# Four residual layers on one core: the start and end of the third stage written out as a list, and two bias additions moved in the first

## The chip, the core and the metric

The kernel runs on one core of one Trainium2 chip. The metric is the device time of one execution in microseconds, the median of several runs. Matmuls run on TensorE (PE), elementwise work on VectorE (DVE), ScalarE (ACT) and GpSimd (POOL), and SyncE (SP) issues most transfers; POOL issues some too.

## The reference

The input x has shape (8192, 8, 16, 16) in fp32. Four layers each add to x a linear map of its group norm (four groups of channels for every sample):

```
x = x + tt_matvec([core0, core1, core2], gn(x)) + bias0             # layer 0
x = x + relu(batchnorm(conv3x3(gn(x)) + bias1))                     # layer 1
g = gn(x);  sx = 127 / max|g|;  sw = 127 / max|w2|
x = x + conv3x3(round(g * sx), round(w2 * sw)) / (sx * sw) + bias2  # layer 2
x = x + conv3x3(edge_pad(gn(x)), sign(w3) * mean|w3|) + bias3       # layer 3
```

Layer 0 is a product of three small cores of rank 8 instead of a full matrix. The batch norm of layer 1 and the largest magnitude in layer 2 need all samples, so there are two points at which everything must be known.

## The kernel before

A tile is 128 samples, so there are 64 tiles (`NT`), each of 128 rows with 2048 values. The two global results cut the work into three stages: the first does layer 0 and the convolution of layer 1 for tile after tile, the second applies the batch norm and finds the largest magnitude, the third does layers 2 and 3. Most of the intermediate tiles go through DRAM between stages; `KEEP` = 13 stay on chip in slots.

PE, DVE, ACT and POOL are called through `InOrder` (line 43), which keeps each engine's instructions in the order in which the Python code issues them. So the order written in the kernel is the order on every engine, nearly all of the rows of the profile carry line 43, and a step that waits holds up whatever stands behind it on its engine.

**The first stage** goes through quarters of tiles: a loop over n = 4t + q. Layer 0 of a quarter is an expansion on PE (`pu`), its copy by ACT (`u`), and the main product on PE (`po`), which DVE adds to the tile (`xs`). The transposed operand of the expansion arrives in two parts, a rounded one (`xh`, by ACT) and the rest (`bs - xh`, by POOL); `limbs(t, q)` makes both and sends them to DRAM (`limb_d`), and `fetch(t, q)`, a transfer that POOL issues, brings them back as `xl`. Around the matmuls of quarter n the loop hangs other steps into slots 0 to 6 with `at(slot, condition, step, ...)`: norms of tiles to come, layer 1 of tiles gone by, and `add_bias(t)`, one POOL addition of bias 0 over the whole tile (128 x 2048). That addition must come before the first `po` of tile t is added to it. For tile 1 it is in quarter 0, for tile 2 in slot 5 of quarter 1, for tile t + 3 in slot 1 of the last quarter of tile t. DVE meanwhile also builds the weights of the later layers (`ys`, `band`, `sign`, `wsum` and others).

**The third stage** is one loop over laps in which eight tiles are under way at different steps. For a tile the steps are, in their order: `rows2` (DVE: the norm's factors as rows) and `spread` (PE: spread over the columns into `ps_a`), `scale2` (DVE: `v`, as int8), `round2` (ACT: `q`, as bf16), `bias2` (ACT, on the first half of x), `layer2` (PE: two halves `pq`; DVE adds the first to x, ACT scales the second into `z` and POOL adds that), `square3` (ACT: `sq`), `stats3` (PE: `s`; DVE: `s_d`, `mv`; POOL: a power of `mv`), `rows3` and `spread` again (`ps_r`, `ps_o`), `offset3` (ACT: `c`), `scale3` (DVE: `t`, in the buffers `sq` and `xh`), `high3` (ACT: `hi` with its edges), `low3` (POOL: `lo` = t - hi, then x + c), `edges3` (ACT), `layer3` (PE: two halves `pf`, each six matmuls with hi and six with lo) and `finish` (DVE; after the second half SP issues the store). In a lap i these steps are called for tiles i + 3 to i - 3 in a fixed sequence, whose start and end are the same lap with the tiles that do not exist left out. The tile that a lap loads from DRAM is i + 7 (`AHEAD`).

Of the kernel before, what the change touches and what calls it, by code (L numbers as in the profile page):

```python
# [18 lines left out]
P = 128  # L19
# [13 lines left out]
class InOrder:  # L33
# [5 lines left out]
    def __getattr__(self, name):  # L39
        op = getattr(self.engine, name)  # L40

        def call(*args, **kwargs):
            return self.tc.keep_in_program_order(op(*args, **kwargs))  # L43
        return call

# [6 lines left out]
def tile_net(ctx: ExitStack, tc: tile.TileContext, xb, xt_in, pack0, pack1, pack2, out):  # L54
# [210 lines left out]
    def samples(t):  # L265
        return t.rearrange("p (b w) -> p b w", w=W)
# [29 lines left out]
    with first as s:  # L296
# [274 lines left out]
        for n in range(NT * NQ):  # L571
            t, q = divmod(n, NQ)
            steps = {}

            def at(r, ok, f, *args):
                if ok:
                    steps.setdefault(r, []).append((f, args))

            def at1(r, f, lag):
                if quarter_of(n, lag):  # L580
                    at(r, True, f, *quarter_of(n, lag))

            last, before, ahead = t == NT - 1, t > 0, t + 2 < NT
            if n > 0:
                next(rest, None)
                if n == 1:
                    next(rest, None)
            tn, qn = divmod(n + 1, NQ)
            at(0, tn < NT, expand, tn, qn, 0)
            at(4, tn < NT, expand, tn, qn, 1)  # L590
            at1(0, conv1_input, LAG)
            if n < NT * NQ - 1:
                at1(6, conv1_scaled, LAG - 1)
            if n == 0 and NT > 1:
                at(1, True, norm_b_spread, 1)
                at(1, True, norm_b_apply, 1)
                at(1, True, add_bias, 1)
            if q == 0:
                if before and t - 1 not in y_of:
                    nc.sync.dma_start(x1_d[t - 1], T[t - 1]["x"])  # L600
                at(1, before, norm_sums, t - 1)
                at(4, before, norm_stats, t - 1)
                if ahead:
                    load_b(t + 2)
            elif q == 1:
                at(1, ahead, norm_b_square, t + 2)
                at(1, before, norm_apply, t - 1)
                at(4, t + 3 < NT, load_t, t + 3)
            elif q == 2:
                at(1, ahead, norm_b_sums, t + 2)  # L610
                at(1, ahead, norm_b_stats, t + 2)
            else:
                at(1, t + 3 < NT, add_bias, t + 3)
                at(1, ahead, norm_b_spread, t + 2)
                at(1, ahead, norm_b_apply, t + 2)
            at1(3, conv1_output, LAG + 1)

            for m in {0: [], 1: [4, 5], 2: [6, 7], 3: []}.get(n, [n + NQ]):
                at(0 if n < 3 else 2, m < NT * NQ, limbs, *divmod(m, NQ))
            for m in {0: [], 1: [4, 5], 2: []}.get(n, [n + 3]):  # L620
                at(5, m < NT * NQ, fetch, *divmod(m, NQ))
            if n == 1:
                at(5, NT > 2, add_bias, 2)
            if last:
                at(2, q > 1, quarter_apply, t, q - 2)
                at(2, q > 0, quarter_stats, t, q - 1)
            main(t, q, steps, n0=QS // 2 if n == 0 else None)
            if quarter_of(n, LAG):
                conv1(*quarter_of(n, LAG))
            if n == NT * NQ - 2 and NT > STAY + 3:  # L630
                load2(STAY)
                load2(STAY + 1)
# [47 lines left out]
    def sums_pe(ps, x, sq):  # L680

        for k, src in ((0, x), (1, sq)):
            for q in range(NQ):
                pe.matmul(ps[32 * q:32 * q + 32], L["wsum"][:, k], src[:, q * BANK:(q + 1) * BANK],
                          start=(k == 0), stop=(k == 1))
# [5 lines left out]
    def stats_small(mv, st, ps, name):  # L691

        s = small.tile([P, 32], F32, name=f"s_{name}", tag="s")
        dve.tensor_reduce(s, samples(ps), AX.X, ALU.add)
        dve.transpose(st, s)
        sq = small.tile([P, G], F32, name=f"sq_{name}", tag="sqm")
        dve.tensor_copy(mv[:, 0:G], st[:, 0:G])
        dve.tensor_tensor(sq, st[:, 0:G], mv[:, 0:G], ALU.mult)
        dve.scalar_tensor_tensor(mv[:, G:2 * G], st[:, G:2 * G], EPS, sq, ALU.add, ALU.subtract)
# [144 lines left out]
    with ExitStack() as s:  # L844
# [5 lines left out]
        sq3, t3, z3 = sqs[0], [sqs[1], xh], [y_stay[3][:, h * F // 2:(h + 1) * F // 2] for h in range(2)]  # L850
        T = [dict() for _ in range(NT)]
        AHEAD = min(NT, KEEP - 6)
        FIRST = 3
        diag2, diag3 = diagonal("d"), diagonal("e")

        ps_a, ps_r, ps_o = (ps_s.tile([P, BANK], F32, name=f"ps_{n}", tag=n) for n in ("a", "r", "o"))
# [4 lines left out]
        def load3(i):  # L861
            t = order[i]
            if t in kept:
                T[i]["x"] = kept[t]
                return
            T[i]["x"] = x_slots[(NT - KEEP + i) % KEEP]
            nc.sync.dma_start(T[i]["x"], x2_d[t])

        def halves(t):
            return t.rearrange("p (h n) -> p h n", h=2)  # L870
# [7 lines left out]
            dve.tensor_tensor(mr, st3[:, 0:G], mv[:, G:2 * G], ALU.mult)  # L878
            T[i]["rows3"] = to_rows(diag3[i % 2], mask, [mr, mv[:, G:2 * G], gnst[:, order[i], 0:G]], f"e{i}")

        def spread(i2, i3):

            if 0 <= i2 < NT:
                pe.matmul(r2, L["sel0"], T[i2].pop("rows2"), start=True, stop=True)
            if 0 <= i3 < NT:
                rows = T[i3].pop("rows3")
                pe.matmul(r3, L["sel1"], rows, start=True, stop=True)
                pe.matmul(o3, L["corr"], rows, start=True, stop=True)

        def scale2(i):  # L890

# [15 lines left out]
        def layer2(i, h):  # L907
            pc = ps_c.tile([P, 2, BANK], F32, name=f"pq_{i}_{h}", tag="pc")
            for k in range(2):
                pv, xv = samples(pc[:, k]), samples(T[i]["q"])[:, (2 * h + k) * QS:(2 * h + k + 1) * QS]  # L910
                pe.matmul(pv, L["band2"][:, 1], xv, start=True, stop=False)
                pe.matmul(pv[:, :, 1:W], L["band2"][:, 0], xv[:, :, 0:W - 1], start=False, stop=False)
                pe.matmul(pv[:, :, 0:W - 1], L["band2"][:, 2], xv[:, :, 1:W], start=False, stop=True)
            pc, x = pc.rearrange("p k n -> p (k n)"), halves(T[i]["x"])[:, h]
            if h == 0:
                dve.scalar_tensor_tensor(x, pc, inv, x, ALU.mult, ALU.add)
            else:
                z = z3[i % 2]
                act.activation(z, pc, AF.Identity, bias=L["bias2"], scale=inv)
                pool.tensor_tensor(x, x, z, ALU.add)  # L920

        def square3(i):
            act.activation(sq3, T[i]["x"], AF.Square)

        def stats3(i):
            ps = ps_s.tile([P, BANK], F32, name=f"s3_{i}", tag="s3")
            sums_pe(ps, T[i]["x"], sq3)
            T[i]["mv"] = small.tile([P, 2 * G], F32, name=f"mv3_{i}", tag="mv")
            stats_small(T[i]["mv"], st3, ps, f"d{i}")
            stats_pow(T[i]["mv"])  # L930

        def offset3(i):
# [19 lines left out]
        def low3(i):  # L952
            hi = T[i]["hi"]
            T[i]["lo"] = lo = wk.tile([P, P, W + 2], F32R, name=f"lo_{i}", tag="lo")
            pool.tensor_tensor(lo[:, :, 1:W + 1], samples(T[i].pop("t")), hi[:, :, 1:W + 1].bitcast(F32), ALU.subtract)
            x = samples(T[i]["x"])
            pool.tensor_tensor(x, x, over_w(T[i].pop("c"), 0, P), ALU.add)

# [14 lines left out]
        def finish(i, h):  # L973
            x = halves(T[i]["x"])[:, h]
            pc = T[i].pop(("pf", h)).rearrange("p k n -> p (k n)")
            dve.scalar_tensor_tensor(x, pc, L["scale3"], x, ALU.mult, ALU.add)
            if h == 1:
                nc.sync.dma_start(out[order[i]], T[i]["x"])
                T[i].clear()

        def at(i, f, *args):
            if 0 <= i < NT:
                f(i, *args)

        for i in range(AHEAD):
            load3(i)
        for i in range(-FIRST, NT + 4):
            at(i + AHEAD, lambda j: j >= AHEAD and load3(j))
            at(i + FIRST, rows2)
            at(i - 1, rows3)  # L990
            at(i - 3, finish, 1)
            at(i, square3)
            at(i + 1, layer2, 0)
            spread(i + FIRST, i - 1)
            at(i - 1, offset3)
            at(i + 1, layer2, 1)
            at(i + FIRST, scale2)
            at(i, stats3)
            at(i - 1, scale3)
            at(i - 2, edges3)  # L1000
            at(i + 2, round2)
            at(i - 1, high3)
            at(i + 2, bias2)
            at(i - 1, low3)
            at(i - 2, layer3, 0)
            at(i - 2, finish, 0)
            at(i - 2, layer3, 1)


# [67 lines left out]
```

## Time and profile before

| what | value |
| --- | --- |
| median of 4 runs | 3845.68 us (3844.68 to 3848.49) |
| profiled execution | 3845.59 us |
| its span | 3843.8 us |
| granted TensorE clock, mean | 0.96 |
| first stage | 0 to about 2607 us |
| second stage | about 2620 to 3070 us |
| third stage | 3070.3 to 3843.8 us |
| PE busy, 130 to 2600 us | all of 2470.0 us |
| PE busy, 3070 to 3123 us | 36.5 of 53.0 us |
| PE busy, 3123 to 3800 us | 673.9 of 677.0 us |
| PE busy, 3800 to 3843.8 us | 34.6 of 43.8 us |

The span is what the hardware profiler saw between the first and the last instruction; the time of the execution lies 1.8 us above it. In the lines of a view the first number is when an instruction starts, in microseconds from the beginning of the span, and the second how long it takes; a name in front of an arrow is what is written, and those behind it are what is read. In brackets stands idle time of the engine just before, with what ended it. `pf` and `po` are the large matmul groups. A row joins neighbouring instructions of one kind where it says x2 or more.

### The profile page before, as it was taken

How to read it: one execution, taken by the hardware profiler on the slowest of the kernel's cores; microseconds unless marked ns; L12 is line 12 of the kernel's file. 1: busy time of each engine (PE TensorE's matmuls, PEld its weight loads, DVE VectorE, ACT ScalarE, POOL GpSimd, SP SyncE). 2: the span in 40 equal slices, each digit the busy share in tenths (PEclk: the TensorE clock that was granted, in tenths of full speed). 3: DMA queues.
4: the chain of work that ended last, by engine and by line, in shares of the span. 5: the costliest groups of instructions: out<-in, count | busy, mean ns of one | idle time of the engine just before them, and what ended most of it. 6: DMA issues, size and time to landing. Idle time of an engine off the chain costs nothing.

```text
span 3843.8 us, 52765 instructions
## 1 busy us (share of the span) xinstructions
PE 3606.2 (94%) x16264; PEld 2126.8 (55%) x16326; DVE 3403.3 (89%) x6313; ACT 2510.9 (65%) x2676; POOL 3049.7 (79%) x3104
## 2 busy tenths in 40 slices
PE   7999999999999999999999999996665589999999
PEld 4666666666666666666666666662211145555555
DVE  8988888888888888888888888877998889999997
ACT  5666666666666666666666666665665477777775
POOL 4877778777777787777877777766887679999998
PEclk9999999999999999999999999997776699999999
DMA  5787787877877878778788887757999624444432
GB/s 211 243 278 256 261 266 250 271 254 263 268 256 261 260 256 275 255 260 267 251 269 253 263 269 257 251 170 307 425 425 425 266 100 185 178 185 187 175 154 99
DMA packets 210809, 960.93 MB, mean 250 GB/s; under 512 B 44896, under 2 KB 45152, under 8 KB 110048
## 3 DMA queue, kind: packets, MB, share of 16 engines
q1 hardware_dynamic: 173808, 692.22, 48.5%
q0 software_dynamic: 36288, 264.26, 23.2%
q8 instruction: 131, 2.15, 0.2%
q14 instruction: 150, 1.23, 0.1%
q10 hardware_dynamic: 432, 1.08, 0.1%
HBM read 578.84 MB, written 378.54 MB: 249 GB/s over the span
## 4 chain that ended last, share of the span: by engine, by line
PE 85%; DVE 7%; DMA 5%; POOL 2%; issue 1%; ACT 0%; POOLq 0%; SPq 0%; DVEq 0%; ACTq 0%
PE po L43 44%; PE pu L43 12%; PE pf L43 10%; PE pm L43 6%; PE pq L43 4%; PE s L43 3%; PE pc L43 3%; DVE top L43 2%; DMA sq<-y_d 1%; DVE ys L43 1%; DMA xs<-x_d 1%; DMA ys<-x_d 1%; DMA u<-x_d 1%; DMA xk<-x_d 1%; DMA x_d<-xs 1%
## 5 line engine op out<-in xcount | busy, mean ns | idle before, releaser
L43 PE MATMUL po<-u,core 128*128 128x512 f32 (+1 forms) x4112 | 1844.0, 591 | 1.7 <-DVE xs L43 1.7
L43 ACT COPY u<-pu 128x2048 f32<-128x2048 f32 x512 | 955.4, 1866 | 514.2 <-PE pu L43 514.0
L43 PEld LDWEIGHTS po<-u,core 128*128 128x128 f32 x4112 | 744.2, 190 | 738.6 <-issue 735.9
L43 PE MATMUL pu<-core2r,xl 128*128 128x256 f32 x4032 | 678.5, 310 | 5.3 <-ACT u L43 4.7
L43 PEld LDWEIGHTS pu<-core2r,xl 128*128 128x128 f32 x4032 | 527.9, 189 | 128.6 <-issue 122.0
L43 POOL TENSOR_TENSOR bs<-bs,xh 128x512 fp32r<-128x512 f32 (+1 forms) x253 | 325.4, 1287 | 203.9 <-ACT xh L43 203.7
L43 POOL TENSOR_TENSOR v<-e 128x128 f32<-128x128 f32 x750 | 396.7, 540 | 0.0
L43 DVE TENSOR_TENSOR xs<-po,xs 128x512 f32<-128x512 f32 x256 | 176.9, 691 | 216.8 <-PE po L43 216.7
L43 ACT ACTIVATE m<-pm,b 128x128 f32<-128x128 f32 x250 | 91.7, 367 | 390.6 <-PE pm L43 390.6
L43 PEld LDWEIGHTS pm<-v,fast 128*128 128x128 f32 x2000 | 262.5, 191 | 119.7 <-issue 107.1
L43 POOL TENSOR_TENSOR e<-x1n,x 128x512 f32<-128x512 f32 x250 | 305.8, 1223 | 23.5 <-ACT x L43 16.0
L43 DVE TENSOR_TENSOR bs<-bs,stat 128x1024 f32<-128x1024 f32 x252 | 290.8, 1217 | 2.1
L43 POOL TENSOR_TENSOR xs<-xs,w 128x2048 f32<-128x2048 f32 x64 | 291.9, 4560 | 0.6 <-DMA xs<-in_xt 0.6
L43 PE MATMUL pm<-v,fast 128*128 128x128 f32 x2000 | 263.5, 275 | 0.0
L43 ACT ACTIVATE x<-x1n 128x512 f32<-128x512 f32 x500 | 247.0, 545 | 2.1 <-DVE x1n L43 2.1
L43 POOL TENSOR_TENSOR mv<-mv,mhalf 128x4 f32<-128x4 f32 x127 | 130.8, 1030 | 139.5 <-DVE mv L43 139.5
L43 PE MATMUL pf<-hi,sign 128*128 128x512 f32 x768 | 227.6, 434 | 0.0
L43 POOL DMA_DIRECT2D xl<-limb_d x252 | 149.8, 594 | 95.5 <-ACT x L43 25.6
L43 PE MATMUL pf<-lo,sign 128*128 128x512 f32 x768 | 220.2, 424 | 2.0 <-ACT lo L43 2.0
L43 POOL TENSOR_TENSOR v<-r 128x128 f32<-128x128 f32 x500 | 215.1, 446 | 0.0
L43 ACT ACTIVATE sq<-xs 128x2048 f32<-128x2048 f32 x103 | 196.7, 1910 | 11.0 <-DVE xs L43 6.3
L43 PE MATMUL gb<-rows_c,sel 128*128 128x128 f32 x128 | 40.5, 411 | 169.0 <-DVE rows_c L43 169.0
(293 smaller groups left out, 7206.5 us busy)
## 6 DMA issues: line engine op xcount, KB each, us to landing
xl<-limb_d POOLq DMA_DIRECT2D x252, 1024.0 KB, 7.4
x_d<-xs SPq DMA_DIRECT2D x76, 1024.0 KB, 8.4
xs<-in_xt SPq DMA_DIRECT2D x64, 1024.0 KB, 7.5
bs<-in_xb SPq DMA_DIRECT2D x63, 1024.0 KB, 5.7
limb_d<-xh SPq DMA_DIRECT2D x1008, 64.0 KB, 4.4
limb_d<-bs SPq DMA_DIRECT2D x1008, 64.0 KB, 5.2
y_d<-ys SPq DMA_DIRECT2D x60, 1024.0 KB, 8.1
u<-x_d SPq DMA_DIRECT2D x36, 1024.0 KB, 6.2
```

Source lines behind the costliest of these rows:

```text
L43: return self.tc.keep_in_program_order(op(*args, **kwargs))
```

## The change

It has two parts.

In the third stage the fixed loop is replaced by a list of pairs (step, tile). Some steps are cut in two so that they can be placed by themselves: `spread` becomes `spread2` and `spread3`; `layer2` leaves the DVE addition to `first2` (in the list `stz`), ACT's part to `second2` (`z1`) and POOL's to `add2` (`add1`); `stats3` becomes `sums3`, `stats3` (`small`) and `pow3`; the second addition of `low3` becomes `add3` (`corr`). The list's middle is `TURN`, the sequence of the lap before. Its first entries are replaced by `C_HEAD`, in which the tiles 0 to 8 occur, and its last ones by `C_TAIL`, in which the tiles are counted from the end. Each step is in the list as often as before.

In the first stage `add_bias(2)` goes from slot 5 of quarter 1 to slot 2 of quarter 4, and `add_bias(3)` from slot 1 of quarter 3 to slot 5 of quarter 5, behind `fetch`.

```diff
+C_HEAD = """
+rows2:0 rows2:1 spread2:0 v:0 rows2:2 spread2:1 bias:0 v:1 q:0 rows2:3 spread2:2 v:2 c2h1:0 c2h0:0 stz:0 spread2:3
+q:1 z1:0 add1:0 v:3 bias:1 c2h0:1 sq:0 c2h1:1 stz:1 z1:1 sums:0 rows2:4 small:0 add1:1 pow:0 spread2:4 rows2:6
+rows3:0 q:2 q:3 sq:1 c2h1:2 c2h0:2 spread3:0 sums:1 z1:2 bias:2 rows2:5 t:0 small:1 hi:0 stz:2 c:0 add1:2 pow:1
+c2h1:3 rows3:1 spread3:1 c2h0:3 v:4 sq:2 lo:0 z1:3 t:1 bias:3 corr:0 sums:2 stz:3 edl:0 hi:1 c:1 small:2 q:4
+spread2:5 c3h0:0 out0:0 c3h1:0 c2h1:4 v:5 add1:3 pow:2 sq:3 rows3:2 out1:0 lo:1 rows2:7 z1:4 spread3:2 t:2 bias:4
...
+C_TAIL = """
...
+add1:-1 out1:-4 out0:-4 hi:-3 sq:-1 c:-3 spread3:-2 sums:-1 lo:-3 corr:-3 c:-2 t:-2 edl:-3 c3h0:-3 small:-1 c3h1:-3
+pow:-1 hi:-2 lo:-2 rows3:-1 out0:-3 spread3:-1 t:-1 edl:-2 hi:-1 c3h0:-2 corr:-2 lo:-1 edl:-1 c:-1 corr:-1 out1:-3
+out0:-2 c3h1:-2 out1:-2 c3h0:-1 out0:-1 c3h1:-1 out1:-1
+""".split()
...
-                at(1, t + 3 < NT, add_bias, t + 3)
+                at(1, before and t + 3 < NT, add_bias, t + 3)
...
-            if n == 1:
-                at(5, NT > 2, add_bias, 2)
+
+            at(2, n == NQ and NT > 2, add_bias, 2)
+            at(5, n == NQ + 1 and NT > 3, add_bias, 3)
...
+        TURN = [("rows2", 3), ("rows3", -1), ("out1", -3), ("sq", 0), ("c2h0", 1), ("stz", 1), ("spread2", 3), ("spread3", -1),
+                ("c", -1), ("c2h1", 1), ("z1", 1), ("add1", 1), ("v", 3), ("sums", 0), ("small", 0), ("pow", 0), ("t", -1),
+                ("edl", -2), ("q", 2), ("hi", -1), ("bias", 2), ("lo", -1), ("corr", -1), ("c3h0", -2), ("out0", -2),
+                ("c3h1", -2)]
+        todo = [(op, i + k) for i in range(-3, NT + 4) for op, k in TURN if 0 <= i + k < NT]
+        if len(todo) >= len(C_HEAD) + len(C_TAIL):
+            head, tail = ([(op, int(i) + n) for op, i in (c.split(":") for c in l)] for l, n in ((C_HEAD, 0), (C_TAIL, NT)))
+            todo = head + todo[len(head):len(todo) - len(tail)] + tail
         for i in range(AHEAD):
             load3(i)
-        for i in range(-FIRST, NT + 4):
-            at(i + AHEAD, lambda j: j >= AHEAD and load3(j))
...
+        for op, i in todo:
+            if op == "rows2" and AHEAD <= i + 4 < NT:
+                load3(i + 4)
+            OPS[op](i)
```

## The prediction

> **What bounds the kernel now.** I read the page's first and fourth parts, then the chain of waits and the timeline where the diff touches: the first 110 us, the start and the end of the third stage.
>
> ```profile
> PE 3606.2 (94%) x16264; PEld 2126.8 (55%) x16326; DVE 3403.3 (89%) x6313; ACT 2510.9 (65%) x2676; POOL 3049.7 (79%) x3104
> ...
> PE 85%; DVE 7%; DMA 5%; POOL 2%; issue 1%; ACT 0%; POOLq 0%; SPq 0%; DVEq 0%; ACTq 0%
> ```
>
> TensorE is 94% busy, and 85% of the chain. So only places where PE is not the chain are open to a new order. The first is the start of stage one, where the chain of waits runs on DVE from about 40 to 97 us:
>
> ```profile
> 50.48 4.63 DVE mvb L43
> ...
> 57.07 4.80 DVE ys L43
> ...
> 96.88 3.70 PE po L43 x8
> ```
>
> The timeline shows what those two DVE steps are (start, duration, engine, operation):
>
> ```profile
> 48.03 4.60 POOL L43 TENSOR_TENSOR xs<-xs,w 128x2048 f32<-128x2048 f32 x1
> ...
> 50.48 4.62 DVE L43 TENSOR_SCALAR mvb<-mvb 128x8 f32<-128x8 f32 x1
> ...
> 56.60 4.84 POOL L43 TENSOR_TENSOR xs<-xs,w 128x2048 f32<-128x2048 f32 x1
> ...
> 57.07 4.79 DVE L43 TENSOR_TENSOR ys<-ys 128x384 f32<-128x384 f32 x1
> ```
>
> The same TENSOR_SCALAR takes 0.17 us at 95.65, and another ys of this shape 0.56 at 61.89. Both stand still beside POOL work on SBUF: `add_bias(2)` at 48.03 with two limb subtractions behind it, and `add_bias(3)` at 56.60. Ten microseconds on, PE pays:
>
> ```profile
> 68.61 1.91 ACT L43 ACTIVATE sq<-xs 128x2048 f32<-128x2048 f32 x1 [6.33 <-DVE xs L43]
> ...
> 70.94 1.86 ACT L43 COPY u<-pu 128x2048 f32<-128x2048 f32 x1
> ...
> 72.85 2.08 PE L43 MATMUL pu<-core2r,xl 128*128 128x256 f32 x8 [4.71 <-ACT u L43]
> ...
> 74.72 4.90 PE L43 MATMUL po<-u,core 128*128 128x512 f32 x8
> ```
>
> DVE's late xs holds ACT's sq, that holds the u copy, PE idles 4.71 us and then runs slow: 2.08 and 4.90 for groups that take 1.50 and 3.60 around 60 us.
>
> The second place is the start of stage three, at the reduction `pm` (3070.33); "+" below counts from there.
>
> ```profile
> 3077.75 1.44 PE L43 MATMUL pq<-q,band 128*128 128x512 bf16 x3 [0.76 <-ACT q L43]
> ...
> 3082.44 1.20 ACT L43 ACTIVATE bs<-pq,bias,inv 128x1024 f32<-128x1024 f32 x1 [3.69 <-PE pq L43]
> ...
> 3083.55 1.89 ACT L43 CAST q<-v 128x2048 bf16<-128x2048 int8 x1
> ...
> 3085.48 2.72 PE L43 MATMUL pq<-q,band 128*128 128x512 bf16 x6 [3.14 <-ACT q L43]
> ...
> 3111.00 1.82 PE L43 MATMUL pf<-hi,sign 128*128 128x512 f32 x6
> ```
>
> ACT's q of tile 1 stands behind the z of tile 0, which waits 3.69 for PE; then PE waits 3.14 for q. From 3111.00 the pf matmuls run and soon a lap takes 11.54 us (PE: ps 0.67, pq 2.7, s 1.85, pf 6.4). The third place is the drain, where POOL rows follow one another:
>
> ```profile
> 3819.60 4.28 POOL L43 TENSOR_TENSOR lo<-sq,hi 128x2048 fp32r<-128x2048 f32 x1 [0.52 <-POOL mv L43]
> ...
> 3823.83 3.69 POOL L43 TENSOR_TENSOR xk<-xk,c 128x2048 f32<-128x2048 f32 x1
> ...
> 3827.49 4.28 POOL L43 TENSOR_TENSOR lo<-xh,hi 128x2048 fp32r<-128x2048 f32 x1
> ...
> 3831.71 3.70 POOL L43 TENSOR_TENSOR ys<-ys,c 128x2048 f32<-128x2048 f32 x1
> ```
>
> **The steady laps: nothing.** `TURN` is the old loop's order with its pieces named, and the engines keep it; the same matmuls, casts and transfers are issued, `load3(i+4)` still with `rows2(i)`. What hides it is PE's 11.54 per lap; POOL's lap (lo 4.27, c 3.69, half 2.42, pow 1.02 = 11.40) is next, 0.14 below. A new start can't change the pitch of lists that wait only on each other, and I saw no stretched DVE row in stage three.
>
> **Stage one: 4.0 us less.** Taking the two adds out of the first tile gives DVE back 4.62 - 0.17 = 4.45 and 4.79 - 0.56 = 4.23: 8.68 us, all on the chain. Part is lost where they are put.
>
> `add_bias(2)` now follows the limb subtraction that POOL did at 71.12. That one waits for ACT's cast, and ACT comes forward less than DVE: its u copy at 60.42 (1.87) stays, then sq 1.91, cast 0.60, POOL's subtraction 1.26: the add runs from about 66.1 to 70.6. DVE's next scalar step of that kind (mv, at 76.47 before) comes 8.7 earlier, at 67.8, and stands 2.8 us. POOL's pow of mv is queued behind the add, but needs that mv anyway.
>
> `add_bias(3)` follows the fetch at 80.87 (0.57 on POOL's queue, so the add would start at 81.44). DVE's copy to `sign` ran at 81.35 for 0.36: a lead of 0.1 us. If the copy wins, nothing is held; if the add is first, DVE stands most of 4.55, some 4.5. Queued behind the add on POOL are e, r and v of the first 3x3 convolution (85.35 before, after 3.91 us of idle time, waiting for ACT): covered unless they come over 3 us earlier.
>
> So DVE's chain gains 8.68 - 2.8 = 5.9, or 1.4 with the copy held. PE's own loss there was 4.71 + 0.58 + 1.30 = 6.6, so it does not cap this much. The middle is 3.7; I take 4.0, as the slow PE groups (1.88) go in both cases. From 97 us on the steady 10.08 us quarters are PE's and carry the shift on.
>
> The Trainium skill (SBUF — State Buffer, Who interferes with whom) says that a GpSimd instruction and a VectorE instruction with two SBUF inputs, or in a two-port mode, exclude each other for the whole length of whichever is first. The 4.79 row agrees, and by it a move saves nothing by itself: the add takes its toll from whatever stands beside it at the new place.
>
> **Start of stage three: 3.9 us less.** What is moved: `rows2` and `spread2` of tiles 1 and 2, v(1) and bias(0) come before the first pq, and q(1) before z(0).
> - First pq. v(0) ends near +5.5 (3.03 + 2.35); v(1) +6.7 to +9.05 as before; `spread2(2)` writes the bank that v(1) reads, and PE holds the pq behind it: +9.5, where before had +7.42. That is 2.1 lost. ACT's bias(0) (1.14) ahead of q(0) ends it at +8.5, covered.
> - Then the four halves of tiles 0 and 1 run without the 3.14 and 3.69 waits: with 8 matmuls at 0.43 and 16 at 0.22 plus one ps_a, PE is through at +17.2.
> - z(0) after the first half (+12.1) 1.2, POOL's half 2.4 to +15.7, sq 1.9 to +17.6, second half of s 1.03: +18.7. Before: 3092.07 + 1.03 = 3093.10, +22.8. Gain 4.1.
> - From there to the first pf before took 17.9 us, of which s_d to lo's edge is some 13.5 on the rows (1.7, pow 1.07, 1.1, t 2.34, hi 2.47, lo 4.27, 0.54). POOL's half of tile 1 (2.4) now stands before pow of tile 0, beside s_d. I keep 17.9, and take 0.2 off for slow s matmuls: 3.9.
>
> The bounds come from the clock. Its view by windows gives 0.50 for 3076.4 to 3081.1, 1.00 to 3084.5 and 0.50 to 3091.3. All 24 first matmuls at 0.43 cost 16 x 0.21 = 3.4 more, gain 0.5; if the 6.4 us of PE waits between 3093 and 3111 shrink by a quarter, gain 5.5.
>
> The Trainium skill (TensorE: Matmul & The Clock Gate, Part 1) says that half speed is given up only after a busy window of about 3.4 us, that the windows run freely, and that the count of slow matmuls varies by run. The stretches of 3.4 us agree; by that rule either end can occur in one run or another.
>
> **Drain: 0.1 us less.** The last 25.23 us of POOL (3810.18 to 3835.41: lo, c, pow, lo, c, lo, c) hold 0.52 of idle time, and `C_TAIL` leaves them in this order. At most 0.5 can go; nothing follows but ACT's edge, pf 4.93, DVE 1.28 and the last store.
>
> Sum: 4.0 + 3.9 + 0.1 = 8.0. The profiled execution took 3845.59 (span 3843.8 and 1.8 around it), 0.09 below the median of four (3845.68): 3845.59 - 8.0 = 3837.6. About 0.2%, 7.7 us, is what a measurement of this kernel tells from no change, so "faster" is below 3838.0, and my forecast sits on the border.
>
> **Rivals.**
> - *Half given back.* The add beats the copy (1.4 instead of 4.0) and the first matmuls stay slow (0.5 instead of 3.9), or one of them with the other part poor: 2 to 5 us in all, 3840.6 to 3843.6. For: a lead of 0.1 us, and half clock in three of the first four windows. Against: PE in the new head has work queued without a break from +9.5.
> - *Fuller gain.* The copy wins (5.9) and the waits up to the first pf shrink (5.5): 11.4, 3834.2. For: 13.5 against 17.9. Against: in-order POOL gets the half of tiles 1 and 2 between.
> - *Slower: late fetches.* The fetches of xl at 98.53 and 109.20 have no cover: the latter lands in 7.65, at 116.85, and PE's pu starts at 116.99. If the moved adds push POOL's queue past its idle time, each add costs PE 4.55 and a slow group like the one at 72.85 (1.9). One add: stage one +6.5 instead of -4.0, with 4.0 gained in stage three a total of +2.5, 3848.1; both: 12.9 - 4.0, 3854.5. It decides when POOL falls behind by more than its waits at 71.12 (9.11), 77.11 (4.74) and 85.35 (3.91), 17.8 us for 9.1 us of adds: unlikely.
> - *It does nothing.* Stage three has no gain if the first pf stays at +40.7 after all; this falls into the first rival, with 3841.5.
>
> **How the numbers follow.** Forecast 0.58 (its own range 3835.5 to 3840.5; 0.38 below 3838.0 and 0.20 above); half given back, with nothing in stage three, 0.20; fuller gain 0.14; late fetches 0.08, of which 0.05 for both adds. Faster 0.38 + 0.14 = 0.52; slower 0.05; same 0.43. The range 3834.0 to 3843.6 leaves out the slower rival, and an edge on either side.
>
> **What would show it.** Right: no DVE row of 4.6 near 50 and 57 us; PE's 4.71 gone; one mv row of about 3 us under the add at 66 to 71; first pf at about +36.8 after the reduction with the first pq at about +9.5; laps of 11.54; the last POOL rows with the same order and spacing. Wrong: a `sign` row over 4 us, a PE wait on xl of microseconds near 100 to 117, laps that differ, or a drain shorter by over 0.5.

## The result

| | before | changed |
| --- | --- | --- |
| median | 3846.12 us (60 runs, 3842.89 to 3848.49) | 3841.78 us (42 runs, 3839.85 to 3845.57) |
| profiled execution, span | 3845.59, 3843.8 us | 3842.75, 3841.0 us |

The changed kernel is 4.3 us faster: the ratio is 0.999 with a 95% interval of 0.9985 to 0.9994, or 2.3 to 5.8 us. The forecast was 3837.6, 8.0 us faster, which lies outside that interval; the measured time lies inside the forecast's range, at the rival called "half given back" (3840.6 to 3843.6). In the terms of the prediction it is "same", less than 7.7 us; with over a hundred runs in the comparison it is nonetheless clear of zero.

The page of the changed kernel, its first and fourth parts, shows how small that is beside the whole:

```profile
PE 3604.7 (94%) x16264; PEld 2127.2 (55%) x16326; DVE 3399.7 (89%) x6313; ACT 2512.4 (65%) x2676; POOL 3048.4 (79%) x3104
...
PE 85%; DVE 6%; DMA 6%; issue 2%; POOL 1%; ACT 1%; POOLq 0%; SPq 0%; DVEq 0%; ACTq 0%
```

**First stage.** The chain of waits of the changed kernel, 40 to 130 us, no longer holds mvb and ys at four to five microseconds. Two other DVE rows stand there, and the transfers follow:

```profile
67.95 2.46 DVE mv L43
...
75.10 4.86 DVE sign L43
...
83.86 1.76 ACT u L43
...
107.10 7.84 DMA xl<-limb_d
```

The timeline of the same stretch shows both additions at their new places and who stands beside them:

```profile
65.83 4.53 POOL L43 TENSOR_TENSOR xs<-xs,w 128x2048 f32<-128x2048 f32 x1
...
67.95 2.45 DVE L43 TENSOR_SCALAR mv<-mv 128x8 f32<-128x8 f32 x1
...
73.34 1.32 POOL L43 TENSOR_TENSOR bs<-bs,xh 128x512 fp32r<-128x512 f32 x1 [0.84 <-ACT xh L43]
...
73.56 1.51 DVE L43 TENSOR_TENSOR band<-ys 128x384 f32<-128x384 f32 x1
...
74.60 0.57 POOL L43 DMA_DIRECT2D xl<-limb_d  x1
75.10 4.86 DVE L43 CAST sign<-band 128x384 fp32r<-128x384 f32 x1
75.19 4.54 POOL L43 TENSOR_TENSOR xs<-xs,w 128x2048 f32<-128x2048 f32 x1
...
85.66 1.21 PE L43 MATMUL pu<-core2r,xl 128*128 128x256 f32 x8 [3.46 <-ACT u L43]
```

The mv row takes 2.45 instead of 0.17, the copy to sign 4.86 instead of 0.36: each stands still until the addition beside it has ended, which is called a hold below. The PE idle time of 4.71 before 72.85 is gone, and a new one of 3.46 stands before 85.66.

**Start of stage three.** From pm (3068.58) the first pq comes at +9.48 (3078.06), the first pf at +37.53 (3106.11; before +40.67). But these first pf groups are slow, 2.91 and 2.76 us where 1.8 and 1.7 is usual. Timeline, and the view by windows (span of the window, then PE busy, PEld, DVE, ACT, POOL, granted clock):

```profile
3101.34 1.04 PE L43 MATMUL s<-sq,wsum 128*32 128x512 f32 x8
3101.83 0.55 ACT L43 CAST lo<-lo 128x256 fp32r<-128x256 f32 x1
...
3105.66 0.80 PE L43 MATMUL ps_a<-rows_d,sel 128*128 128x128 f32 x2 [3.28 <-DVE mv L43]
3106.11 2.91 PE L43 MATMUL pf<-hi,sign 128*128 128x512 f32 x6
3108.81 2.76 PE L43 MATMUL pf<-lo,sign 128*128 128x512 f32 x6
```

```profile
3096.40:3099.80 3.40, 1.28 (x8) 0.92 (x9) 3.33 (x9) 3.37 (x5) 3.40 (x3) 1.00 0.00 0
3099.80:3103.20 3.40, 2.58 (x20) 0.53 (x18) 3.40 (x4) 2.75 (x4) 3.40 (x2) 1.00 0.00 0
3103.20:3106.60 3.40, 0.94 (x3) 0.93 (x4) 2.27 (x6) 3.37 (x4) 3.40 (x2) 0.74 0.00 0
3106.60:3110.00 3.40, 3.40 (x9) 2.63 (x8) 0.00 (x0) 2.84 (x2) 3.40 (x3) 0.50 0.00 0
```

The last operand of the first pf, the edge of lo of tile 0, is ready at 3102.38 (the CAST row). PE stands another 3.28 us, waiting for DVE's mv, ahead of the `spread2(5)` that the written list puts in front of this pf.

**Drain.** The last POOL row now has idle time in front, and what ends it is an ACT row that follows the edge of lo:

```profile
3824.40 4.27 POOL L43 TENSOR_TENSOR lo<-xh,hi 128x2048 fp32r<-128x2048 f32 x1
...
3828.71 0.53 ACT L43 CAST lo<-lo 128x256 fp32r<-128x256 f32 x1 [4.75 <-POOL lo L43]
3829.14 0.35 ACT L43 ACTIVATE c<-ps_o,bias 128x128 f32<-128x128 f32 x1
...
3829.57 3.69 POOL L43 TENSOR_TENSOR ys<-ys,c 128x2048 f32<-128x2048 f32 x1 [0.90 <-ACT c L43]
```

### The profile page after: what moved, and what is told of

Read it like the earlier page. It is cut to its first block, busy times and chain, and to the rows that moved or that the text cites. A ratio compares the mean times of both kernels' runs of the same rounds, so it can differ in the third digit from the quotient of the medians.

```text
span 3841.0 us, 52769 instructions
## 1 busy us (share of the span) xinstructions
PE 3604.7 (94%) x16264; PEld 2127.2 (55%) x16326; DVE 3399.7 (89%) x6313; ACT 2512.4 (65%) x2676; POOL 3048.4 (79%) x3104
## 4 chain that ended last, share of the span: by engine, by line
PE 85%; DVE 6%; DMA 6%; issue 2%; POOL 1%; ACT 1%; POOLq 0%; SPq 0%; DVEq 0%; ACTq 0%
PE po L43 45%; PE pu L43 12%; PE pf L43 10%; PE pm L43 6%; PE pq L43 4%; PE s L43 3%; PE pc L43 3%; DVE top L43 2%; DMA yk<-y_d 2%; DMA x_d<-xs 1%; DMA xs<-x_d 1%; DMA x_d<-xk 1%; DMA xk<-x_d 1%; DMA u<-x_d 1%; DVE xs L43 0%
## 5 line engine op out<-in xcount | busy, mean ns | idle before, releaser
L43 PE MATMUL po<-u,core 128*128 128x512 f32 (+1 forms) x4112 | 1842.7, 591 | 2.2 <-DVE xs L43 2.2
L43 ACT COPY u<-pu 128x2048 f32<-128x2048 f32 x512 | 955.4, 1866 | 515.4 <-PE pu L43 515.2
L43 PEld LDWEIGHTS po<-u,core 128*128 128x128 f32 x4112 | 743.6, 190 | 738.3 <-issue 735.0
L43 PE MATMUL pu<-core2r,xl 128*128 128x256 f32 x4032 | 677.6, 310 | 5.1 <-ACT u L43 3.5
L43 PEld LDWEIGHTS pu<-core2r,xl 128*128 128x128 f32 x4032 | 527.1, 189 | 128.4 <-issue 123.1
L43 POOL TENSOR_TENSOR bs<-bs,xh 128x512 fp32r<-128x512 f32 (+1 forms) x253 | 325.2, 1286 | 200.3 <-ACT xh L43 200.3
L43 POOL TENSOR_TENSOR v<-e 128x128 f32<-128x128 f32 x750 | 396.8, 540 | 0.0
L43 DVE TENSOR_TENSOR xs<-po,xs 128x512 f32<-128x512 f32 x256 | 177.0, 691 | 217.8 <-PE po L43 217.6
L43 ACT ACTIVATE m<-pm,b 128x128 f32<-128x128 f32 x250 | 91.7, 367 | 395.8 <-PE pm L43 395.8
L43 PEld LDWEIGHTS pm<-v,fast 128*128 128x128 f32 x2000 | 262.5, 191 | 119.7 <-issue 106.0
L43 POOL TENSOR_TENSOR e<-x1n,x 128x512 f32<-128x512 f32 x250 | 305.7, 1223 | 26.2 <-ACT x L43 18.7
L43 DVE TENSOR_TENSOR bs<-bs,stat 128x1024 f32<-128x1024 f32 x252 | 290.8, 1217 | 2.1
L43 POOL TENSOR_TENSOR xs<-xs,w 128x2048 f32<-128x2048 f32 x64 | 291.5, 4554 | 0.7 <-DMA xs<-in_xt 0.7
L43 PE MATMUL pm<-v,fast 128*128 128x128 f32 x2000 | 263.5, 275 | 0.0
L43 ACT ACTIVATE x<-x1n 128x512 f32<-128x512 f32 x500 | 247.0, 544 | 7.6 <-DVE x1n L43 7.6
L43 POOL TENSOR_TENSOR mv<-mv,mhalf 128x4 f32<-128x4 f32 x127 | 130.7, 1029 | 139.2 <-DVE mv L43 138.8
L43 PE MATMUL pf<-hi,sign 128*128 128x512 f32 x768 | 228.2, 435 | 0.1
L43 PE MATMUL pf<-lo,sign 128*128 128x512 f32 x768 | 220.6, 424 | 2.2 <-ACT lo L43 2.2
L43 POOL DMA_DIRECT2D xl<-limb_d x252 | 149.7, 594 | 89.9 <-ACT x L43 26.7
L43 POOL TENSOR_TENSOR v<-r 128x128 f32<-128x128 f32 x500 | 215.2, 446 | 0.0
L43 POOL TENSOR_TENSOR mvb<-mvb,mhalf 128x4 f32<-128x4 f32 x64 | 66.3, 1036 | 168.8 <-DVE mvb L43 168.8
L43 ACT ACTIVATE sq<-xs 128x2048 f32<-128x2048 f32 x103 | 196.8, 1910 | 4.9 <-POOL xs L43 4.9
```

## The experiments

Run times of one kernel spread over 2 to 6 us, so three distances in each trace carry the comparison: when DVE adds the first po of tile 20 (stage one in its steady quarters), from pm to POOL's lo of tile 54 (start of stage three and its laps), and from that lo to the last store (the drain). All times in us.

| kernel | po sum of tile 20 | pm to lo 54 | lo 54 to last store | median (runs) |
| --- | --- | --- | --- | --- |
| before | 841.85 | 659.44 | 108.92 | 3846.12 (60) |
| changed | 839.93 | 657.79 | 109.47 | 3841.78 (42) |
| e1, additions only | 841.36 | 659.42 | 108.93 | 3844.87 (11) |
| e2, list only | 842.44 | 655.65 | 109.41 | 3844.34 (11) |
| e3, list's start only | 841.93 | 655.86 | 108.91 | 3844.02 (11) |
| e4, list's end only | 843.49 | 659.38 | 109.46 | 3846.90 (11) |
| e5, add 3 in quarter 9 | 836.69 | 655.69 | 109.46 | 3837.25 (11) |
| e6, add 3 in quarter 6 | 842.38 | 657.60 | 109.46 | 3843.41 (10) |
| e7, PE kept busy | 840.44 | 655.28 | 109.46 | 3841.88 (11) |
| e8, three edits | 837.22 | 655.14 | 109.17 | 3836.85 (11) |
| e9, only add 2 moved | 838.28 | 656.25 | 109.42 | 3840.10 (10) |
| e10, only add 3 moved | 837.65 | 656.09 | 109.31 | 3840.17 (10) |

Kernels with the same stage one differ by up to 1.6 in the first column (841.85 to 843.49 with the additions as before, mean 842.4; 839.93 to 841.36 with the change's, mean 840.6); in the second column the old start repeats to 0.1 and the written one to 1.1, but for two values near 657.7 (the changed kernel and e6), of which below; the third repeats to 0.2 for each kind of end.

The first four split the change. The kernel before ran beside them at 3846.10 (33 runs).

**e1, additions only.** The list's head and tail are not put in, so `TURN` runs throughout:

```diff
-            todo = head + todo[len(head):len(todo) - len(tail)] + tail
```

> Only the two bias additions are moved; the third stage runs in the old lap order throughout. Theory A (the copy to sign stands behind the add, and the stage passes on what its trace showed, 1.9 us at the po group of 118.17): total -1.5 to -2.2 us, sign row above 4 us, the reduction pm near 3068.5. Theory B (the forecast's term, as if the copy had won): -4 us, sign row 0.36, pm near 3066. Theory C (the total is decided by the phase of the clock windows at the start of stage three, not by the parts): the total differs from the shift of pm by 1 us or more.

The DVE row of sign in e1's timeline, with the POOL rows around it:

```profile
76.05 0.57 POOL L43 DMA_DIRECT2D xl<-limb_d  x1
76.55 4.86 DVE L43 CAST sign<-band 128x384 fp32r<-128x384 f32 x1
76.64 4.54 POOL L43 TENSOR_TENSOR xs<-xs,w 128x2048 f32<-128x2048 f32 x1
```

Again sign is held for 4.86, with the same 0.09 between its start and the add's. The median is 1.2 below before, the mean of the runs 1.8, so the 1.5 to 2.2 of Theory A holds for the mean only; pm came only at 3070.11, 1.5 later than in the changed kernel with the same first two stages: that is the spread between executions. Theory B is out because sign was not free; the times alone would not exclude its 4 us (95% interval of the ratio 0.9987 to 1.0005). Theory C is not what this trace shows: pm and the total are both 0.22 below before, and the distances behind pm are those of before to 0.02.

**e2, list only**, and **e3, the list's start only**:

```diff
-            at(2, n == NQ and NT > 2, add_bias, 2)
-            at(5, n == NQ + 1 and NT > 3, add_bias, 3)
+            if n == 1:
+                at(5, NT > 2, add_bias, 2)
...
-                at(1, before and t + 3 < NT, add_bias, t + 3)
+                at(1, t + 3 < NT, add_bias, t + 3)
...
-            todo = head + todo[len(head):len(todo) - len(tail)] + tail
+            todo = head + todo[len(head):]                              # e3
```

> Only the third stage's written list; the additions stand where they stood before. Theory A (list gains its start, gives back in the drain): first pf 3.1 to 3.7 us earlier from pm than before, steady laps 1.7 to 3.7 earlier by how the first pf is clocked, last POOL row with an idle 0.9 before it, total -1.2 to -3. Theory B (forecast): -4.0. Stage one as before: pm near 3070.3, DVE rows of 4.6 and 4.8 at 50 and 57 us.

> The written start of the list alone, the end in the old lap order, additions as before. Theory A (the written end costs): 0.3 to 0.7 us faster than the list with both ends, no idle before the last POOL row. Theory B (the end gains 0.1): 0.1 us slower than with both ends.

Both gain 3.6 to 3.8 from pm to lo 54, twice what the changed kernel's trace shows (1.65). The first pf in e2's PE timeline says why:

```profile
3109.30 1.81 PE L43 MATMUL pf<-hi,sign 128*128 128x512 f32 x6
3110.94 1.71 PE L43 MATMUL pf<-lo,sign 128*128 128x512 f32 x6
```

The first pf starts at +37.49, as in the changed kernel (+37.53), but at full speed. So in the traces the list's start is worth 3.7, or 1.65 in an execution whose clock is low at that moment. e3 leaves out the written end and its drain is 108.91, that of before, with no idle time ahead of the last POOL row.

The run times show less. The medians of e2 and e3 are 1.8 and 2.1 below before, where the traces would give 3.2 and 3.7, and neither interval excludes zero. Runs with a slow first pf may be among them; how many is not on record.

**e4, the list's end only**, with the additions as before:

```diff
-            todo = head + todo[len(head):len(todo) - len(tail)] + tail
+            todo = todo[:len(todo) - len(tail)] + tail
```

> The written end of the list alone. Theory A (offset c of the last tile is put behind the edge of lo on ACT, and POOL waits 0.9 for it, while PE's last pf runs sooner): +0.2 to +0.7 us against before. Theory B: -0.1. In the trace: the last three POOL rows with or without an idle of 0.9.

The drain is 109.46 against 108.92, and the last POOL row carries `[0.89 <-ACT c L43]` (0.90 in the changed kernel). Theory A: the written end costs 0.5. (Its median is 0.8 above before; runs of this spread don't tell that from 0.5.)

The next four ask what the changed kernel gave back; the kernel before ran beside them at 3845.80 (33 runs).

**e5 and e6, add_bias(3) elsewhere.**

```diff
-            at(5, n == NQ + 1 and NT > 3, add_bias, 3)
+            at(1, n == 9 and NT > 3, add_bias, 3)      # e5
+            at(1, n == 6 and NT > 3, add_bias, 3)      # e6, behind conv1_input
```

> The changed kernel with add_bias(3) in slot 1 of quarter 9 instead of slot 5 of quarter 5, so that nothing on POOL stands beside DVE's copy to sign. Theory A (the lost race is what the first stage gave back): sign row 0.36 instead of 4.86, the po sums of tile 20 1.5 to 3 us earlier than in the changed kernel's trace (839.93), total 1.5 to 3 us below it. Rival (the transfer chain of xl holds PE anyway at 100 to 117 us): sign row 0.36, but tile 20 within 0.7 us of 839.93 and the total the same.

> The same addition in slot 1 of quarter 6, behind the e, r and v of the first 3x3 convolution and ahead of POOL's power of tile 3's norm and its limbs. Theory A alone (only the hold matters): sign row 0.36 and as fast as with quarter 9. The forecast's late-fetch rival: sign row 0.36, but POOL's limbs and the fetches of xl near 97 and 107 us come later, PE waits on xl or xs there for some 2 to 4 us more, and tile 20 is 1 to 4 us later than with quarter 9, that is, no better than the changed kernel or worse.

In e5's timeline sign is free, and at 85 us nothing stands beside it:

```profile
76.67 0.36 DVE L43 CAST sign<-band 128x384 fp32r<-128x384 f32 x1
...
85.02 0.35 DVE L43 COPY sel<-mod 128x128 f32<-128x128 f32 x2
...
91.94 3.70 PE L43 MATMUL po<-u,core 128*128 128x512 f32 x8 [1.47 <-DVE xs L43]
```

Tile 20 is 3.2 us earlier and the median 4.5 below the changed kernel's, more than the 1.5 to 3 expected; against before it is 8.55 less, a ratio of 0.9979 (0.9970 to 0.9988). Theory A. In e6 the addition met the next copy:

```profile
85.04 4.75 DVE L43 COPY sel<-mod 128x128 f32<-128x128 f32 x2
85.06 4.52 POOL L43 TENSOR_TENSOR xs<-xs,w 128x2048 f32<-128x2048 f32 x1
...
96.36 5.62 PE L43 MATMUL po<-u,core 128*128 128x512 f32 x8 [5.83 <-DVE xs L43]
```

Both expectations for e6 had the mechanism wrong. Theory A's form of it (as fast as e5) failed; the late-fetch rival had the outcome (5.7 us later at tile 20), but PE waits for xs from DVE and not for xl. It is the same hold on another copy, which I had not looked for: sel 4.75 instead of 0.35.

**e7, PE kept busy.** A step before `spread2(5)` issues 20 matmuls into the buffer of the first pf, which the pf then overwrites:

```diff
+        def busy(i):
+            T[i]["early"] = pc = ps_c.tile([P, 2, BANK], F32, name=f"pf_{i}_0", tag="pc")
+            for _ in range(20):
+                pe.matmul(pc[:, 0, 0:2 * P].rearrange("p (a n) -> p a n", a=2), L["band2"][:, 1], L["band2"][:, 0:2], start=True, stop=True)
...
-spread2:5 c3h0:0 out0:0
+busy:0 spread2:5 c3h0:0 out0:0
```

> The changed kernel with 20 matmuls of 128 columns by 256 that nobody reads, on PE ahead of spread2(5), where PE idled 3.28 us before the first pf. Theory A (the first pf groups ran at half clock because of that idle window, and this cost the laps 2.1 us: pm to lo of tile 54 took 657.8 here and 655.7 with the list alone): first pf rows 1.8 and 1.7, pm to lo of tile 54 655.5 to 656.3, total on average 0.3 to 1.5 us below the changed kernel, since only some runs have the slow pf. Rival (the slow pf is made up by the laps that follow): 657.8 stays.

```profile
3103.13 2.36 PE L43 MATMUL pf<-band 128*128 128x256 bf16 x20
3106.47 0.49 PE L43 MATMUL ps_a<-rows_d,sel 128*128 128x128 f32 x2 [0.99 <-DVE mv L43]
3106.72 1.79 PE L43 MATMUL pf<-hi,sign 128*128 128x512 f32 x6
3108.34 1.71 PE L43 MATMUL pf<-lo,sign 128*128 128x512 f32 x6
```

In the trace it does what Theory A says: idle time 0.99 instead of 3.28, pf at full speed, pm to lo 54 at 655.28. In the times it hardly shows: the median is 0.1 above the changed kernel's, the mean 0.3 below (3841.63 to 3841.91). The runs are closer together, 3840.6 to 3842.3, but there are 11 of them against 42.

The granted clock in all traces with the written start, taken in steps of 1 us (an edge is worked out from the mean clock of the step that it lies in), tells why some have a slow first pf. Times are us from pm:

| trace | full clock from | half clock | first pf |
| --- | --- | --- | --- |
| changed | 12.4 | 36.2 to 43.1 | 37.5, slow |
| e6 | 12.1 | 36.0 to 42.8 | 37.5, slow |
| e2 | 13.4 | 30.5 to 33.9 | 37.5 |
| e3 | 14.3 | 31.3 to 34.8 | 37.9 |
| e5 | 13.6 | 30.6 to 34.0 | 37.6 |
| e9 | 15.1 | 32.1 to 35.6 | 38.1 |
| e10 | 14.4 | 31.5 to 34.9 | 38.0 |
| e7, e8 (extra matmuls) | 12.0, 11.8 | none | 37.3, 37.1 |

All seven traces without the extra matmuls fall to half clock once here. In five the stretch ends before the first pf, where PE has time to spare; in the changed kernel and e6 (first pf groups of 2.91 and 2.74) it covers the pf. From the first full clock to the fall it is 17.1 us in the five and 23.9 in the two, that is five and seven times 3.41. So the clock changes at the ends of windows of 3.41 us, and these stand differently to the program in each trace, though the order is the same. In the window before each fall PE was busy for 0.96 to 1.45 us; no window at full clock with 1.46 us or more, in these traces and in that of before, was followed by a fall. In e7 and e8 the extra matmuls fill the window that held 0.96 and 1.22 in the two slow traces. How often the changed kernel's runs have the slow pf stays open: it is two traces of seven.

**e8, three edits**: e5 and e7, and in the written end

```diff
-pow:-1 hi:-2 lo:-2 rows3:-1 out0:-3 spread3:-1 t:-1 edl:-2 hi:-1 c3h0:-2 corr:-2 lo:-1 edl:-1 c:-1 corr:-1
+pow:-1 hi:-2 lo:-2 rows3:-1 out0:-3 spread3:-1 c:-1 t:-1 edl:-2 hi:-1 c3h0:-2 corr:-2 lo:-1 edl:-1 corr:-1
```

> Three edits in the changed kernel: add_bias(3) in quarter 9, the 20 matmuls of the run before, and in the written end the offset c of the last tile right behind its spread instead of behind the edge of lo. Theory A (the three losses are independent and add up): no idle before the last POOL row, lo of tile 54 to the last store 108.9 us (109.5 in the changed kernel), pm to lo of tile 54 near 655.9, tile 20 near 838, total 3 to 5 us below the changed kernel, 3837 to 3839. If one of them is no loss of its own, its part is missing from the sum.

```profile
3818.56 4.29 POOL L43 TENSOR_TENSOR lo<-xh,hi 128x2048 fp32r<-128x2048 f32 x1
...
3822.81 3.69 POOL L43 TENSOR_TENSOR ys<-ys,c 128x2048 f32<-128x2048 f32 x1
```

POOL's idle time is gone and the drain is 109.17, 0.3 shorter, not 0.5: the end is then set by the last pf and DVE's addition after it. The median, 3836.85, is the lowest of all here, 8.95 below before (ratio 0.9980, 0.9971 to 0.9988) and 4.9 below the changed kernel, but 4.5 of that e5 has alone; the 0.4 between the two is less than the spread of either.

**e9 and e10, one addition moved.** The kernel before ran beside them at 3846.11 (19 runs).

```diff
-            at(5, n == NQ + 1 and NT > 3, add_bias, 3)             # e9: 3 in quarter 3 again
+                at(1, t + 3 < NT, add_bias, t + 3)
...
-            at(2, n == NQ and NT > 2, add_bias, 2)                 # e10: 2 in quarter 1 again,
+            at(5, n == 1 and NT > 2, add_bias, 2)
+            at(1, n == 9 and NT > 3, add_bias, 3)                  #      3 in quarter 9
```

> The changed kernel with add_bias(3) back in quarter 3; of the two additions only that of tile 2 is moved. Theory A (what counts is the rows that stand beside an addition, each for the length of the hold): mvb 0.17 instead of 4.6 near 50, one hold of about 4.3 near 53 to 57 or on whatever stands beside the addition there, mv held up to 2.3 or not, sign 0.36; tile 20 between 838.5 and 841.5, so no worse than the changed kernel although one hold is back. Rival (the two moves only help together, since DVE waits for POOL either way): tile 20 near 842.4 as before.

> The changed kernel with add_bias(2) back in quarter 1 and add_bias(3) in quarter 9; of the two only that of tile 3 is moved, to where nothing on DVE is held by it. Theory A: mvb held 4.4 as before, ys 0.56, no hold on mv and sign; DVE gains 4.2 over before with nothing given back: tile 20 at 837 to 839. Rival (both must leave): tile 20 near 842.

The timelines of e9 (first two lines) and of e10 show one long hold each. Sign is free in both (0.36); mv is free in e10 (0.17) and takes 0.47 in e9:

```profile
52.66 4.83 POOL L43 TENSOR_TENSOR xs<-xs,w 128x2048 f32<-128x2048 f32 x1
...
53.13 4.78 DVE L43 TENSOR_TENSOR ys<-ys 128x384 f32<-128x384 f32 x1
```

```profile
48.37 4.61 POOL L43 TENSOR_TENSOR xs<-xs,w 128x2048 f32<-128x2048 f32 x1
...
50.68 4.77 DVE L43 TENSOR_SCALAR mvb<-mvb 128x8 f32<-128x8 f32 x1
```

They are 6.0 and 5.9 us below before, with one of the two holds still there: better than the change, which took both out and put in two others. Tile 20 comes 4.1 and 4.8 earlier than with the additions as before (mean 842.4), e5 with both out and none in but mv's (2.27) 5.7. Added up, the two single gains less mv's hold would be 6.6. The 0.9 between lies within the 1.6 by which traces with the same stage one differ, so these runs do not settle whether some of it is lost to the transfers of xl, for which PE waits 0.40 in e5's timeline (111.83) and 2.70 in e9's (80.62).

## Why the forecast was right and where it failed

- **The holds in the first tile: right.** mvb 4.62 became 0.17, ys 4.79 became 0.56, and PE's 4.71 before 72.85 went.
- **add_bias(2): right.** Said to run from 66.1 and to hold mv 2.8; it ran from 65.83 and held it 2.28.
- **add_bias(3) and sign: the step that failed.** "A lead of 0.1 us" was taken for a race with two outcomes, and the term for the stage was set between them, at 4.0. The rows speak against a race: the subtraction on POOL (73.34 to 74.66) holds DVE's band, which ends 0.41 after it and lets sign follow, and the same subtraction is followed by POOL's fetch and the add. So their distance repeats: 0.09 us in the changed kernel, in e1, in e7 and between the rows that the prediction itself cites (81.35 and 81.44). (In e4's trace, with the additions as before, the fetch waits 0.46 more for PE, and the distance would be 0.58.) The lead was there, and sign was held all the same in the three traces in which the add follows that fetch. The stage gained 1.4 by the lower end worked out there, 1.9 at tile 20 in the traces of before and changed, 1.8 between the means of their kinds. e5, in which sign is free, gained 5.5 (842.4 to 837.0, with e8), near the other end, 5.9.
- **The start of stage three: right up to the sums, then near by luck.** First pq forecast at +9.5, measured +9.48; end of tile 0's sums +18.7, measured +19.1. For the way from there to the first pf the prediction kept 17.9 us, and 18.5 were measured, but not by the chain it named: that chain, to the edge of lo, takes 14.7, and the rest is PE standing ahead of `spread2(5)`. The first pf comes 3.1 earlier than before (+37.53 against +40.67; +36.8 was forecast), not 3.9. Another 0.6 come behind it, in the laps that the list still writes out (first pf to lo of tile 54: 618.8 before, 617.9 to 618.2 in the traces with the list and a fast pf), where the prediction had nothing. Together that is 3.7 in the mean of e2 and e3, and 3.2 to 3.8 over the five traces with a fast pf and no extra matmuls.
- **The clock: foreseen, at another place.** The trace of the changed kernel is the case of the slow clock at a place that I had not named, not the first pq but the first pf: 1.65. The Trainium skill (TensorE: Matmul & The Clock Gate, Part 1) says that an idle window brings the half speed and that the windows run freely. The traces agree, but the window need not be empty: each one ahead of a fall holds 0.96 to 1.45 us of PE work. The first full clock comes between +11.8 and +15.1 with the same order.
- **The drain: wrong in sign, small.** 0.1 less forecast, 0.5 more measured. I compared POOL's order, which is unchanged; on ACT c of the last tile had moved behind the edge of lo, and POOL's last addition needs c.
- **The steady laps: right.** Behind the written start all kernels keep the same pitch, and laps are 11.54 (3333.79 to 3345.33 in the changed kernel, lo to lo).
- **Late fetches:** not seen in the changed kernel, where PE waits for xl 0.81 at 77.59 and at 115.07; nor did e6, set up for them, show them. In e9 and e10 PE does wait for xl, 2.70 and 2.07 us near 80.

The parts sum to 1.85 + 3.7 - 0.5 = 5.0 with a fast first pf and to 3.0 with a slow one; the profiled pair differs by 2.8, the medians by 4.3. With e5's stage one: 5.5 + 3.7 - 0.5 = 8.7, measured 8.55. The forecast's 8.0 would have been about right for a kernel whose third addition stands elsewhere. That the measured time lies in the forecast's range is owed to the rival "half given back", which set that side of the range: its first condition, the add ahead of the copy, came true. Its second, a poor start of stage three, came in part, by another stretch of slow clock than the one it named.

## What to carry to other kernels

When work is moved off a place where it holds up another engine, list what runs beside it at the new place, and look at every instruction there of the kinds that were held at the old one: e6 freed the sign copy and caught the sel copy. When two engines' steps are 0.1 us apart, follow both back to what releases them; if it is the same event, their distance repeats and there are no odds to halve. Which of the two is then held, their starts do not tell. And an order written out by hand has to be compared on every engine: the drain was lost on ACT, with POOL's list unchanged.

## What the runs showed of the hardware that I had not expected

An instruction's start in the trace does not settle who holds whom. Sign's row starts 0.09 us ahead of the addition's (75.10 and 75.19; e1: 76.55 and 76.64), yet it ends 0.23 us after the addition does (79.96, 79.73): it waited for all of it. In the trace of the kernel before another pair has the same lead, and there the POOL row is the longer one:

```profile
79.20 0.56 DVE L43 TENSOR_TENSOR ys<-w,she 128x384 f32<-128x384 f32 x1
...
79.29 1.62 POOL L43 TENSOR_TENSOR bs<-bs,xh 128x512 fp32r<-128x512 f32 x1 [0.55 <-ACT xh L43]
```

ys keeps its usual 0.56, and the subtraction takes 1.62 where the one at 71.12 takes 1.26. The Trainium skill (SBUF — State Buffer, Who interferes with whom) gives the pair of ports to whoever issues first for the whole instruction. These rows agree with the whole length; the moment of issue the trace does not show, and the start does not stand for it.

Tiny operands make no difference. A TENSOR_SCALAR on 128 x 8 values, 0.17 us alone, ended 0.04 us after the addition beside it (mv: 70.40, 70.36). In e10 mvb stood through the rest of an addition and through both subtractions behind it (to 55.45; they end at 55.42). Reductions beside an addition ran on (s at 64.65 in 2.33, the usual time, with the addition of 65.83 beside it).
